# Layer 3 of a graph network: the attention sums moved behind the W_out step, and what follows them moved with them

## The chip, the cores and the metric

The kernel runs on one core of a Trainium2 chip. The metric is the device time of one execution in microseconds (us). The kernel before has a median of 2066.45 us in 3 runs (2065.35 to 2071.23).

## The reference

Four layers work on 32 images of 512 nodes with 64 features each. Layers 0 to 2 are not touched by the change. Layer 3 is a graph attention with 8 heads of width 128, followed by a second attention with one head of width 64 on the heads' output:

```
def gat_layer(x, graph, W, b):
    h = x @ W
    s = einsum('bnd,bmd->bnm', h, h) * graph
    s = where(s == 0.0, -1e16, s)
    a = softmax(s, axis=2)
    return einsum('bnm,bmd->bnd', a, h) + b

h = maximum(layernorm(x), 0)
heads = vmap(gat_layer)(Wh, bh)                 # 8 heads
cat = leaky_relu(concatenated heads, 0.01)
out = gat_layer(cat, graph, W_out, b_out)
x = x + leaky_relu(out, 0.01)
```

All numbers are float32.

## The kernel before

Layer 3 is cut into units. A unit is two attention matrices of 512 x 512 that are worked on side by side: for a `Heads` unit two heads of one image, for an `Out` unit the second attention of two images. There are 128 Heads units and 16 Out units, 144 in all. An Out unit is placed 7 or more units behind the last head that it needs; the last 8 units of the list are Out units.

The order of the instructions on all five queues is written out by hand: `period(t)` (inside `planned`, L702) is called for t = -1, 0, 1, ... and issues one step each of several units. `unit(lag)` is the unit that began `lag` periods ago, `now` is `unit(0)` and `ahead` is `unit(-1)`, the next one. The scheduler keeps this order on each engine, and adds the waits that the data and the buffers ask for. An engine takes its instructions in this order only. `ROOM = 6` periods after the last unit let it finish.

The steps of one unit, with the lines of the kernel before:

- `scores(r)` (L370, PE): for a block r of 128 rows, two score matrices of 128 x 512 into a PSUM tile of tag "s". This tag has two buffers of two banks.
- `maxima(r)` (L382, VectorE): masks the scores, negates them, keeps them in SBUF (`p`), and takes each row's extreme into `top`. Four row blocks give 8 instructions. Blocks 0 and 1 are done a period ahead, 2 and 3 in the unit's own period.
- `spread_out` and `spread_in` (L389, L392, L398): VectorE transposes `top`; four DMAs on SP write it to DRAM as a row, and one DMA on SP reads the row back to all 128 partitions (`topb`, 512 KB).
- `shift(r)` (L404, POOL): subtracts `topb` from a row block of `p`. The order of the blocks is 0, 2, 1, 3.
- `exps(r)` (L413, ACT): the exponential. Blocks 0 and 2 stay in SBUF, blocks 1 and 3 go to a PSUM tile of tag "s".
- `join(r)` for r = 1, 3 (L416, VectorE): adds block r to block r - 1. With it the values can be formed from differences of neighbours' features.
- `values(j)` (L422, PE): the attention's product with the features, four steps, into `av`.
- `totals` (L434, L440): PE sums the joined blocks 1 (e = 0) and 3 (e = 1) over the rows with a matrix of ones, into a PSUM tile; ACT copies it to SBUF (`tot`). This tile has tag "m" (two buffers) before.
- `totals_out` (L445): two small DMAs rearrange the sums to `parts`, one on ACT's queue and one on SP's.
- `recips`, `recips_out`, `recips_in` (L451, L454, L458, L465): VectorE adds the parts and takes reciprocals; a DMA on SP writes them to DRAM as a row; two DMAs on SP read them back to 64 partitions each (`recb`, 128 KB each).
- `normalize` (L471, VectorE): `av` times `recb` gives `o_att`.
- Heads: `y_pe` (L552, PE) multiplies with the head's weights into two tiles of tag "m"; `y_act` (L562, ACT) makes 0.01 times the value plus bias; `y_dve` (L570, VectorE) takes the larger of the two, which is the leaky relu.
- Out: `y_act` (L638, ACT) adds b_out in the kernel before; `back` (L643 PE, L648 ACT) transposes back and makes the 0.01 branch; `back_dve` (L651, VectorE) takes the larger; `back_pool` (L657, POOL) adds x; `store` (L664, SP) writes the result.
- `product(h)` (L597, PE): the W_out step, which gathers 8 heads of two images into `gT_ps`; `keep_product` copies it. `make_v` (L610), `make_gs` (L620), `judge_product` (L623) prepare an Out unit.
- `features`, `make_hx` (L298), `make_g` (L534, L546) prepare Heads units some periods ahead; `any_zero` gathers a test of the inputs' form, in the period after the last unit.

The period before issues on PE: scores of blocks 2 and 3 of `now`, sums of unit(2), scores of blocks 0 and 1 of `ahead`, y of unit(4), values of unit(2), W_out, then make_v, hx and g.

## Time and profile before

| | |
|---|---|
| median of the runs | 2066.45 us |
| the profiled execution's own time | 2070.2 us |
| its span, from the first to the last instruction | 2068.4 us |
| PE busy in the span | 1982.9 us |
| VectorE (DVE) busy | 1774.3 us |
| POOL busy | 1432.8 us |
| ACT busy | 1220.4 us |
| mean granted TensorE clock | 0.985 |
| start of the maxima of blocks 2, 3 of the first, third and last unit | 457.20, 478.12, 2019.60 us |

The busy times are of one profiled execution. A line of the timeline has the start in us from the span's start, the time, the engine, the line of the kernel, the operation, what is written from what, the number of instructions merged, and in brackets the idle time before it with what ended it. PEld is PE's loading of weights, which runs beside its matmuls. "SPq" and "ACTq" are DMA issues on SP's and ACT's queues.

### The profile page before, as it was taken

The numbers are of one execution on the slowest core, as the hardware profiler recorded it, in microseconds if no ns is written. First come the engines' busy times: TensorE is split into PE (matmuls) and PEld (weight loads), VectorE is DVE, ScalarE is ACT, GpSimd is POOL, SyncE is SP. The second block draws the span as 40 slices with busy tenths as digits, with TensorE's granted clock in tenths as the row PEclk, the third lists the DMA queues.
The fourth block names the chain that finished last, engine by engine and source line by source line (L and its number), as shares of the span: only waits on it lengthen the run. The fifth ranks groups of instructions, "written<-read, shape, count | busy, mean of one in ns | idle before, by whom it ended". The sixth has DMA issues, their size and how long they took to land. (4 is left out here: it accounts for less than half of the span.)

```text
span 2068.4 us, 32906 instructions
## 1 busy us (share of the span) xinstructions
PE 1982.9 (96%) x11038; PEld 808.1 (39%) x11038; DVE 1774.3 (86%) x4257; ACT 1220.4 (59%) x1944; POOL 1432.8 (69%) x697
## 2 busy tenths in 40 slices
PE   7999999997999999999999999999999999999995
PEld 4676776762333333333333333333333333333231
DVE  6699997676998889998989898989898898888993
ACT  3444443345666666766666667666666766666553
POOL 2000000008888989898888889888888888888995
PEclk9999999989999999999999999999999999999997
DMA  5000000001222222222222222222222222222222
GB/s 141 1 1 1 1 2 1 2 11 58 78 74 79 74 78 81 76 75 82 74 79 73 83 74 79 73 80 77 69 78 73 69 78 77 75 68 79 76 81 69
DMA packets 135778, 129.32 MB, mean 63 GB/s; under 512 B 92792, under 2 KB 98080, under 8 KB 135472
## 3 DMA queue, kind: packets, MB, share of 16 engines
q1 hardware_dynamic: 116368, 126.35, 20.5%
q10 hardware_dynamic: 18720, 0.59, 0.5%
q8 instruction: 88, 1.44, 0.3%
q0 software_dynamic: 512, 0.20, 0.1%
q14 instruction: 90, 0.74, 0.1%
HBM read 119.48 MB, written 5.37 MB: 60 GB/s over the span
## 5 line engine op out<-in xcount | busy, mean ns | idle before, releaser
L404 POOL TENSOR_TENSOR p_att<-p_att,topb 128x1024 f32<-128x1024 f32 x576 | 1347.8, 2375 | 202.1 <-DMA topb<-top_row 136.7
L382 DVE CUSTOM_DVE_ANT_0 p_att<-s_ps,flow_neg 128x512 f32<-128x512 f32 x1152 | 726.2, 686 | 74.4 <-PE s_ps L370 73.0
L370 PE MATMUL s_ps<-hx,g 64*128 64x512 f32 x2048 | 518.1, 615 | 21.8 <-DVE p_att L416 19.4
L413 ACT ACTIVATE p_att<-p_att 128x1024 f32<-128x1024 f32 x288 | 304.3, 1057 | 232.6 <-POOL p_att L404 219.9
L416 DVE TENSOR_TENSOR p_att<-e_ps,p_att 128x1024 f32<-128x1024 f32 x288 | 342.4, 1200 | 55.4 <-ACT e_ps L413 54.1
L413 ACT ACTIVATE e_ps<-p_att 128x1024 f32<-128x1024 f32 x288 | 295.1, 1028 | 122.1 <-POOL p_att L404 111.2
L370 PEld LDWEIGHTS s_ps<-hx,g 64*128 64x128 f32 x2048 | 174.9, 186 | 336.7 <-DVE top L382 170.5
L422 PE MATMUL av<-p_att,hd 128*64 128x512 f32 x1024 | 270.5, 607 | 0.4 <-DVE o_att L471 0.4
L422 PE MATMUL av<-p_att,hn 128*64 128x512 f32 x1024 | 264.0, 594 | 0.0
L1053 POOL TENSOR_TENSOR x<-x,bias_b 128x512 f32<-128x512 f32 x16 | 20.3, 1274 | 280.7 <-DVE hn L826 280.7
L570 DVE SCALAR_TENSOR_TENSOR cat<-y_ps,bh,cat 128x512 f32<-128x512 f32 x256 | 179.8, 744 | 0.0
L562 ACT ACTIVATE cat<-y_ps,bh 128x512 f32<-128x512 f32 x256 | 161.5, 682 | 30.1 <-PE y_ps L552 28.9
L434 PE MATMUL tot_ps<-p_att,ones 128*32 128x512 f32 x1152 | 154.0, 607 | 0.0
L552 PE MATMUL y_ps<-o_att,wh_sb 64*128 64x512 f32 x512 | 133.0, 590 | 0.0
L597 PE MATMUL gT_ps<-cat,wo_sb 128*64 128x512 f32 x512 | 131.6, 592 | 0.0
L422 PEld LDWEIGHTS av<-p_att,hn 128*64 128x64 f32 x1024 | 73.7, 137 | 146.9 <-issue 146.9
L422 PEld LDWEIGHTS av<-p_att,hd 128*64 128x64 f32 x1024 | 62.3, 136 | 166.6 <-issue 130.1
L977 PE MATMUL acc<-v,s 64*128 64x65 f32 x2048 | 123.8, 279 | 0.7 <-DVE s L963 0.4
L977 PEld LDWEIGHTS acc<-v,s 64*128 64x128 f32 x2048 | 120.9, 194 | 5.9 <-DVE o L993 1.2
L884 PE MATMUL nt_ps<-adj_t,hn 128*128 128x512 f32 x256 | 117.0, 600 | 0.8 <-DVE hn L848 0.8
L471 DVE TENSOR_TENSOR o_att<-av,recb 128x512 f32<-128x512 f32 x144 | 95.4, 663 | 23.8 <-DMA recb<-rec_row 23.1
L546 ACT COPY g<-g_ps 128x512 f32<-128x512 f32 x128 | 69.4, 589 | 71.6 <-PE g_ps L534 71.6
(181 smaller groups left out, 1987.0 us busy)
## 6 DMA issues: line engine op xcount, KB each, us to landing
topb<-top_row SPq DMA_DIRECT2D x144, 512.0 KB
recb<-rec_row SPq DMA_DIRECT2D x288, 128.0 KB
top_row<-top_t SPq DMA_DIRECT2D x576, 1.0 KB
out_dram<-y SPq DMA_DIRECT2D x32, 128.0 KB
x<-in_x_dram SPq DMA_DIRECT2D x3, 1024.0 KB
parts<-tot ACTq DMA_DIRECT2D x144, 4.0 KB
parts<-tot SPq DMA_DIRECT2D x144, 4.0 KB
rec_row<-rec_flow SPq DMA_DIRECT2D x144, 4.0 KB
```

Of the source, the lines that this page charges most:

```text
L370: nc.tensor.matmul(ps[:, k], lhsT=g[halves(k), r * P : (r + 1) * P], rhs=x[halves(k), :], start=True, stop=True,)
L382: nc.vector.tensor_tensor_reduce(out=self.p[r][:, k], in0=ps[:, k], in1=flow_neg[:, r], scale=-1.0, scalar=BIG, op0=OP.add, op1=OP.min, ac ...
L404: nc.gpsimd.tensor_tensor(self.p[r], self.p[r], self.topb, OP.subtract)
L413: nc.scalar.activation(to, self.p[r], AF.Exp, scale=-1.0)
L416: nc.vector.tensor_tensor(self.p[r], self.joined, self.p[r - 1], OP.add)
L422: nc.tensor.matmul(self.av[halves(k), :], lhsT=self.v(k, j) if j % 2 else self.less_next(k, j), rhs=self.p[j][:, k], start=(j == 0), stop= ...
L434: nc.tensor.matmul(ps[q : q + 32, :], lhsT=ones, rhs=self.p[2 * e + 1][:, k], start=True, stop=True,)
L552: nc.tensor.matmul(ps, lhsT=wh_sb[halves(k), 2 * self.i + k, :], rhs=self.o[halves(k), :], start=True, stop=True,)
L562: nc.scalar.activation(self.cat[:, k], self.y[k], AF.Identity, bias=bh01[:, h : h + 1], scale=0.01)
L570: nc.vector.scalar_tensor_tensor(self.cat[:, k], self.y[k], bh[:, h : h + 1], self.cat[:, k], op0=OP.add, op1=OP.max,)
L597: nc.tensor.matmul(self.gps[halves(k), :], lhsT=wo_sb[:, h, :], rhs=Heads.cat.pop((self.b + k, h)), start=(h == 0), stop=(h == H - 1),)
L977: nc.tensor.matmul(self.acc[k][:, r], lhsT=self.s[b // 2][halves(k), b % 2, r * P : (r + 1) * P], rhs=self.v[halves(k), b], start=(b == 0) ...
```

## The change

The change rewrites the order in `period`, and the steps that it moves:

- The sums of a unit (`totals`, `totals_out`) move from the second period after it, behind the first scores, to the first period after it, behind the joins, which on PE is behind the W_out step. Their PSUM tile has tag "s" now. Both DMAs of `totals_out` are on SP, behind `store`.
- `recips`, `recips_out` and `recips_in` of unit(2) come behind the transpose of `now`; the DMA of `recips_out` is issued by ACT, and `recips_in` stands behind `spread_in` on SP.
- `y_pe` and `y_act` take unit(3) instead of unit(4), and stand behind the scores of `now`. `y_dve`, `back_dve` (unit(3)) and `normalize` (unit(2) instead of unit(3)) stand behind the second join.
- Adding b_out is a step of its own, `bias`, at the start of the period. `back` takes unit(3), `back_pool` unit(4).
- The first three `features` steps come ahead of `store` and the second join in the text; on ACT they stand between the last exponential and the copy of the sums.
- `shift(0)` and `exps(0)` of a unit are issued at the end of its own period instead of at the start of the next. For the first unit (t = 1) all four shifts are on VectorE, behind the maxima.

```diff
-        def shift(self, r):
-            nc.gpsimd.tensor_tensor(self.p[r], self.p[r], self.topb, OP.subtract)
+        def shift(self, r, engine):
+            engine.tensor_tensor(self.p[r], self.p[r], self.topb, OP.subtract)
...
         def totals(self):
-            ps = ps_m.tile([P, N], F32, name="tot_ps", tag="m")
+            ps = ps_s.tile([P, 2, N], F32, name="tot_ps", tag="s")[:, 0]
...
-        def totals_out(self, e, queue):
+        def totals_out(self):
 
             rows = self.tot.rearrange("(k e r) n -> k e r n", k=2, e=2)
-            queue.dma_start(
-                self.parts[:, e], rows[:, e, 0].rearrange("k (g i) -> k g i", i=8)
-            )
+            for e in range(2):
+                nc.sync.dma_start(
+                    self.parts[:, e], rows[:, e, 0].rearrange("k (g i) -> k g i", i=8)
+                )
...
         def recips_out(self):
             self.rec_row = dram.tile([2, N], F32, name="rec_row")
-            nc.sync.dma_start(
+            nc.scalar.dma_start(
                 self.rec_row.rearrange("k (g i) -> (k g) i", i=8), self.rec
             )
...
-        def y_act(self):
+        def bias(self):
             nc.scalar.activation(self.o, self.o, AF.Identity, bias=b_out2, scale=1.0)
...
             for r in range(2, C):
                 now.scores(r)
-            unit(3).recips_in()
-            unit(1).shift(0)
-            unit(1).exps(0)
-            unit(2).totals()
-            unit(2).totals_out(1, nc.scalar)
+            unit(3).bias()
+            if t != 1:
+                unit(1).shift(2, nc.gpsimd)
+                unit(1).exps(2)
             u, h = products.get(t - 1, (None, 0))
             if u and h == H - 1:
                 u.keep_product()
-            unit(1).shift(2)
-            unit(1).exps(2)
+            unit(3).y_pe()
+            unit(3).back()
+            unit(3).y_act()
             for r in range(2, C):
                 now.maxima(r)
             now.spread_out()
-            unit(2).totals_out(0, nc.sync)
+            unit(2).recips()
+            unit(2).recips_out()
             now.spread_in()
+            unit(2).recips_in()
             for r in range(2):
                 ahead.scores(r)
-            unit(4).y_pe()
-            unit(4).y_act()
-            unit(3).normalize()
             for r in range(2):
                 ahead.maxima(r)
-            unit(4).back()
-            unit(4).y_dve()
-            unit(4).back_dve()
-            unit(1).shift(1)
-            unit(1).exps(1)
+            if t == 1:
+                for r in (0, 2, 1, 3):
+                    unit(1).shift(r, nc.vector)
+                    if r < 3:
+                        unit(1).exps(r)
+            else:
+                unit(1).shift(1, nc.gpsimd)
+                unit(1).exps(1)
             for j in range(C):
                 unit(2).values(j)
             u, h = products.get(t, (None, 0))
             if u:
                 u.product(h)
-            unit(2).recips()
-            unit(2).recips_out()
             unit(1).join(1)
-            unit(1).shift(3)
+            if t != 1:
+                unit(1).shift(3, nc.gpsimd)
             unit(1).exps(3)
-            unit(5).back_pool()
+            unit(4).back_pool()
             unit(-2).make_gs()
+            for step in range(3):
+                for lag, odd in ((step - 7, 0), (step - 11, 1)):
+                    u = unit(lag)
+                    if getattr(u, "i", None) == 0 and u.b % 2 == odd:
+                        u.features(step)
             unit(5).store()
             unit(1).join(3)
+            unit(3).y_dve()
+            unit(3).back_dve()
+            unit(2).normalize()
+            unit(1).totals()
+            unit(1).totals_out()
             unit(-3).features(3)
             unit(-2).judge_product()
             unit(1).make_v()
             unit(-4).make_hx()
             unit(-2).make_g()
-            for step in range(3):
-                for lag, odd in ((step - 7, 0), (step - 11, 1)):
-                    u = unit(lag)
-                    if getattr(u, "i", None) == 0 and u.b % 2 == odd:
-                        u.features(step)
+            if t:
+                now.shift(0, nc.gpsimd)
+                now.exps(0)
             if t == len(units):
                 any_zero()
```

More of the change, by code (lines that the diff above doesn't have):

```diff
@@ L345, in y_pe @@
             pass
+        def bias(self):
+            pass
         def y_act(self):
@@ L635, in less_next, with bias @@
             return self.gD[:, j // 2, halves(k)]
-        def y_act(self):
+        def bias(self):
             nc.scalar.activation(self.o, self.o, AF.Identity, bias=b_out2, scale=1.0)
```

## The prediction

> **What bounds the kernel now.** I read the table of busy shares and the slices first, then the groups of PE, then the timelines of single engines over two periods of layer 3. Layer 3 fills the time from about 455 us to the end, 144 units in as many periods. In the page PE is the fullest engine there, with POOL behind it:
>
> ```profile
> PE 1982.9 (96%) x11038; PEld 808.1 (39%) x11038; DVE 1774.3 (86%) x4257; ACT 1220.4 (59%) x1944; POOL 1432.8 (69%) x697
> ...
> PE   7999999997999999999999999999999999999995
> ```
>
> The busy times over 478.1 to 2019.6 us (from unit 2's maxima to unit 143's) say it closer: PE 1512.92 of 1541.50 us in 141 periods, so a period is 10.93 us, of which 10.73 are PE's. The period is PE's work, nearly gap for gap. One period on PE:
>
> ```profile
> 1208.46 1.99 PE L370 MATMUL s_ps<-gs 64*128 64x512 f32 x8
> 1210.38 1.06 PE L434 MATMUL tot_ps<-p_att,ones 128*32 128x512 f32 x8
> 1211.37 1.99 PE L370 MATMUL s_ps<-hx,g 64*128 64x512 f32 x8
> 1213.19 1.02 PE L552 MATMUL y_ps<-o_att,wh_sb 64*128 64x512 f32 x4
> 1214.15 1.08 PE L422 MATMUL av<-p_att,hd 128*64 128x512 f32 x4
> ...
> 1217.63 1.03 PE L597 MATMUL gT_ps<-cat,wo_sb 128*64 128x512 f32 x4
> 1218.59 1.13 PE L534 MATMUL g_ps<-hx,m 64*128 64x512 f32 x4
> 1219.55 1.88 PE L370 MATMUL s_ps<-hx,g 64*128 64x512 f32 x8
> ```
>
> The first column is the start, the second the time. W_out (gT_ps) ends near 1218.6. The reader is to hold that against the second join of the same period, in VectorE's timeline; POOL's and ACT's give what leads to it:
>
> ```profile
> 1198.92 0.69 DVE L382 CUSTOM_DVE_ANT_0 p_att<-s_ps,flow_neg 128x512 f32<-128x512 f32 x1 [0.51 <-PE s_ps L370]
> ...
> 1201.48 0.21 DVE L389 STREAM_TRANSPOSE top_t<-top 128x32 f32<-128x32 f32 x1
> ...
> 1218.69 1.22 DVE L416 TENSOR_TENSOR p_att<-e_ps,p_att 128x1024 f32<-128x1024 f32 x1 [0.54 <-ACT e_ps L413]
> ```
>
> ```profile
> 1208.23 9.37 POOL L404 TENSOR_TENSOR p_att<-p_att,topb 128x1024 f32<-128x1024 f32 x4 [1.34 <-DMA topb<-top_row]
> ```
>
> ```profile
> 1217.63 1.03 ACT L413 ACTIVATE e_ps<-p_att 128x1024 f32<-128x1024 f32 x1 [1.20 <-POOL p_att L404]
> ```
>
> This is one unit's way: its maxima of rows 2, 3 start at 1198.92; the transpose ends at 1201.69; the row goes out and comes back, and POOL starts at 1208.23; its four shifts end at 1217.60; exp to 1218.66; the second join to 1219.91. That is 20.99 us, and no piece waits for another engine's queue. Taken the same way for units 10 to 129 the median is 20.95, and the smallest of all units 20.38. So the second join ends 1.3 us after W_out has ended on PE, and 0.36 us after the next unit's scores began. Before, nothing on PE needs it that early: the sums follow one period later.
>
> **What the Trainium skill says.** "PSUM — Partial Sum Buffer", section "Engine vs sequencer instructions": queues are strict FIFO, and matmuls start and complete in program order, so PE can't take the next scores past a sum that waits. The trace agrees so far: PE stands still behind such a wait (17.7 us in all ahead of back_ps, for o_att) with other work queued. "Perfetto Trace Analysis", section "Identifying the Most-Contended Engine": matmul busy time is no measure of the distance to the roofline. I use PE's busy time only as the length of its queue. "DMA: Bandwidth & Descriptors", section "Issuing engines are not separate DMA queues": issuing from another engine saves only the sequencer's issue time. Here that is 0.34 us (rec_row on SP); the 2.02 us from its issue (1206.37) to recb's (1208.39) stay.
>
> **The change, part by part.**
>
> *Sums behind W_out (totals, lag 2 to 1).* PE's new order is: scores 2, 3; y; scores 0, 1 of the next unit; values; W_out; sums of the unit just joined; hx, g or gV; next scores. The work is the same, but a wait is added: sums for e=1 need the second join, and the whole PE queue stands behind it, first of all the next period's scores, from which that unit's maxima come. Two periods thus close a loop. Its parts:
> - maxima to second join: 20.85 (median 20.95; POOL gets slack, so a little less; the ends are 20.4 and 21.2).
> - join to PE: 0.05.
> - sums for e=1: 0.9. All eight take 0.99; the pair for e=0 runs ahead, but the pair left is four instructions like the av group's (1215.06 to 1215.91, 0.85). The ends are 0.5 and 1.0.
> - hx, g, gV before the next scores: hx 0.6 x32, g 0.96 x64, gV 0.6 x16, over 144 = 0.63; g shares PSUM tag m with y, whose largest-of-two now runs after the join (0.74 x2), so its second matmul can wait some 0.3 us; 0.7 in all. The ends are 0.63 and 1.4 (g falls on every other period, and if neighbours can't even it out the loop with it rules).
> - scores start to maxima start: 1.1 (1219.55 to 1220.62, 1208.46 to 1209.63).
> Sum 23.6, so 11.8 us a period against 10.93: +0.87. From unit 3 to unit 143 are 140 periods: +122 us.
>
> *What could hide this?* PE's queue before the sums is 9.2 us long, so nothing covers the wait. Its cover today is the period between join and sums, and that is what the change gives up.
>
> *Sums in ps_s.* Seven tiles of tag s a period instead of six, with two buffers. Scores of row 3 now wait for the copy of the sums on ACT. Sums end + 0.2 + 0.58 (copy) against one scores pair, 0.96: covered. features stands ahead of that copy now (about 1.3 us from the end of exp 3; the join takes 1.22 and the sums 0.9): covered, and costs some 0.3 us in the few periods with two steps of it. I take 0.
>
> *parts, both on SP behind store.* 2 x 0.57 us of issue. They leave spread_out's neighbourhood, where one lay between top_row and topb; but topb was issued 0.32 us after it (1214.61 to 1214.93), waiting for top_row's landing. I take 0 for that, 0.3 as the best. parts lands some 2 us after issue, about 0.5 us before recips stands at the head of VectorE: covered; if late, the maxima of rows 0, 1 start later, and those have 2 us until the joins.
>
> *recips to behind the transpose, rec_row on ACT behind y_act, recb right after topb on SP.* ACT's queue gains 0.5 us; exp 1 behind it has its shift at about the same time. recb stands behind topb, 512 KB. From the second shift: exp 1.05, cat 1.27, issue 0.5, landing 1.5, recb issue and landing 4.3 (2053.26 to 2057.03 in the last unit, 3.8, and 0.5 for topb), division 0.65. With maxima to second shift 13.8 that is 23.1 to the next-but-one maxima, 0.5 us under the loop: covered, but next in line.
>
> *Largest-of-two and division behind the joins.* 2 x 0.7 + 0.6 us on VectorE between join 3 and maxima: 20.85 + 2.0 = 22.9, under 23.6: covered by the sums, hx/g and scores on PE.
>
> *Bias early, shift 0 at the period's end.* POOL's cyclic order is unchanged. The 17.7 us that PE stands before back_ps vanish only where PE sets the period; here they are inside the new wait: 0.
>
> *Ramp.* Unit 0's four shifts move to VectorE. Price by "VectorE: DVE Perf Modes", section "The TRN2 errata — SBUF-src ops pay a fixed extra latency per instruction", (N+151)/0.96 for a fp32 tensor_tensor: an estimate of 1.22 us for N=1024; no row shows this one, the join's 1.20 us with a PSUM operand is near. 4.9 us instead of POOL's 9.26; the ends are 4.4 and 6. The second join of unit 0 ends near 475.2 instead of 478.2, and unit 1's shifts need no longer queue: unit 3's maxima come at 462.68 + 23.6 = 486.3 instead of 489.38: -3.1.
>
> *Tail.* Last unit: maxima 2019.60, span's end 48.8 later. Its sums' copy ended 27.7 after the maxima, because PE had earlier values and back to do. Now it is join 20.9 + 0.9 + 0.8 = 22.6; from there the chain is the same but for 0.6 us of the second issue: -5.
>
> *Sum.* 122 - 3 - 5 = +114 on the profiled 2070.2 us (span 2068.4), that is 2184. The median of the runs is 3.75 lower, 2066.45: **2180 us**.
>
> **Rivals.**
> - *Faster.* If the join came within 2 x 10.73 - 2.75 = 18.7 us of the maxima, PE would not wait: the period falls to PE's 10.73, taking out the 28.6 us that PE idles between 478.1 and 2019.6, with ramp and tail 2066 - 28 - 8 = 2030 us. One mechanism, topb landing 2.1 us sooner with parts out of its way on SP. For it: POOL waits for topb in most periods (1.34 us above). Against: topb waits for top_row, not for SP, and no unit of 144 is under 20.38. 5%.
> - *Milder.* All low ends: 20.4 + 0.05 + 0.5 + 0.7 + 1.1 = 22.75, 11.4 a period, +63 - 8: about 2121 us. 16%.
> - *Heavier.* g and PSUM tag m in one of the two loops, or recb late by a microsecond and division holding the maxima: 24.6, 12.3 a period, +192 - 8: about 2250 us. 15%.
> - *No effect.* The order of the instructions would have to come out as before on PE; it doesn't, the sums do stand behind W_out. Gains and waits cancel by accident: 2%.
>
> **How the numbers follow.** The forecast, 2150 to 2215, has 62%; the milder case fills 2110 to 2150, the heavier 2215 to 2260. Leaving out the faster cases and half the heavier gives 2115 to 2235. Faster by over 0.3% (about what a measurement of this kernel can tell from no change, 6 us) 0.05, within 0.02, slower 0.93.
>
> **What would show it.** Right: PE's idle time ahead of tot_ps with the join (L416's successor) as releaser, about 1 us a period; PE's busy share in layer 3 near 91%; maxima to join still near 20.9; POOL waiting for topb about 2 us a period; cat's wait for y gone. Wrong: the join under 19 us from the maxima, or PE idle ahead of scores (PSUM, copy of the sums) or VectorE idle ahead of recips or division (parts, recb) instead of ahead of tot_ps.

## The result, and the profile after

The changed kernel takes 2259.82 us (median of 4 runs, 2247.58 to 2261.84) against 2066.09 us before on the same chip (2065.35 to 2071.23): ratio 1.0917, 95% interval 1.0879 to 1.0954. The direction was forecast, the size was not: 2180 us was the forecast, and the result lies above its range, where the rival "heavier" had put 2250 us.

The profiled execution has a span of 2256.5 us. First the page's lines on TensorE's busy time and its slices:

```profile
PE 2103.6 (93%) x11038; PEld 863.6 (38%) x11038; DVE 1787.9 (79%) x4261; ACT 1226.1 (54%) x1944; POOL 1421.2 (63%) x693
...
PE   7999999979999999999999999999989999999996
```

PE is busy 120.7 us more than before with the same 11038 matmuls. The profile models where a matmul ends, so part of a matmul's wait for a late operand is counted as busy time. The groups of instructions show where, first of the kernel before, then of the one after. After the first bar stand the busy time in us and the mean time of one instruction in ns; after the second, the idle time in us just before the group, and who ended most of it.

```profile
L434 PE MATMUL tot_ps<-p_att,ones 128*32 128x512 f32 x1152 | 154.0, 607 | 0.0
```

```profile
L437 PE MATMUL tot_ps<-p_att,ones 128*32 128x512 f32 x1152 | 247.4, 608 | 77.8 <-DVE p_att L419 69.3
```

The sums took 154.0 us of PE and now take 247.4 + 77.8 = 325.2: 171 us more, of a span that grew by 188.1. The join (L419) ends the wait. Here is one period in PE's timeline (start, us, engine, line; in brackets the idle time before it); hold it against the PE lines in the prediction:

```profile
1210.17 1.99 PE L373 MATMUL s_ps<-hx,g 64*128 64x512 f32 x8
1211.99 1.02 PE L556 MATMUL y_ps<-o_att,wh_sb 64*128 64x512 f32 x4
1212.88 2.35 PE L373 MATMUL s_ps<-hx,g 64*128 64x512 f32 x8
...
1218.65 1.03 PE L601 MATMUL gT_ps<-cat,wo_sb 128*64 128x512 f32 x4
1219.61 1.05 PE L437 MATMUL tot_ps<-p_att,ones 128*32 128x512 f32 x4
1221.71 1.05 PE L437 MATMUL tot_ps<-p_att,ones 128*32 128x512 f32 x4 [1.05 <-DVE p_att L419]
1222.69 1.46 PE L538 MATMUL g_ps<-hx,m 64*128 64x512 f32 x4
1223.66 2.21 PE L373 MATMUL s_ps<-hx,g 64*128 64x512 f32 x8
```

And this is VectorE's timeline for the unit that meets those sums:

```profile
1200.50 0.69 DVE L385 CUSTOM_DVE_ANT_0 p_att<-s_ps,flow_neg 128x512 f32<-128x512 f32 x1 [1.15 <-PE s_ps L373]
...
1220.43 1.22 DVE L419 TENSOR_TENSOR p_att<-e_ps,p_att 128x1024 f32<-128x1024 f32 x1 [1.10 <-ACT e_ps L416]
1221.57 1.40 DVE L574 SCALAR_TENSOR_TENSOR cat<-y_ps,bh,cat 128x512 f32<-128x512 f32 x2
1222.89 0.68 DVE L475 TENSOR_TENSOR o_att<-av,recb 128x512 f32<-128x512 f32 x1
1225.05 0.69 DVE L385 CUSTOM_DVE_ANT_0 p_att<-s_ps,flow_neg 128x512 f32<-128x512 f32 x1 [1.47 <-PE s_ps L373]
```

The maxima start at 1200.50 and the second join ends at 1221.65: 21.15 us. The second half of the sums starts on PE when the join ends, then come g and the scores, and the maxima of the next unit but one start at 1225.05: 24.55 us for two periods. That is the forecast's loop, with both halves longer. Over units 10 to 129 two periods take 24.68 us in the mean: 21.41 from maxima to second join, 3.27 from there to the maxima (before: 21.17 and 0.70). A line of POOL and two of SP's queue show one reason for the first half:

```profile
1209.99 7.02 POOL L407 TENSOR_TENSOR p_att<-p_att,topb 128x1024 f32<-128x1024 f32 x3 [4.30 <-DMA topb<-top_row]
```

```profile
1205.54 0.34 SPq L401 DMA_DIRECT2D topb<-top_row  x1
1205.98 1.18 SPq L469 DMA_DIRECT2D recb<-rec_row  x2
```

From topb's issue to the start of POOL, which waits for it, the median is 4.28 us; before, when recb was not issued right behind it, it was 3.85. The waits from 600 to 2000 us (who waited, for whom: us in total, times, longest) name the others:

```profile
PEld tot_ps L437 <- DVE p_att L419: 186.7, 161, 2.2
...
ACT e_ps L416 <- DVE top L385: 59.9, 75, 1.8
...
DVE o_att L475 <- DMA recb<-rec_row: 50.8, 48, 3.0
PEld g_ps L538 <- DVE cat L574: 39.4, 47, 0.8
```

The exponentials to PSUM wait for maxima that free their tile, the division waits for recb, and g waits for a PSUM buffer that the larger-of-two (cat) frees.

**An account of TensorE.** Every step of a period passes through PE's one queue, so a mean period can be written as the sum of what each step holds PE: its modelled busy time and the idle time ahead of it, each moment counted once (from the trace, 600 to 2000 us, in us; W_out is in "values"; the last column holds the Out units' transposes and gV). Such a sum comes out for any kernel. It shows at which step PE's time went; why it went there is for the waits and the experiments to say.

| kernel | period | sums | scores | y | g | HX | values | transposes |
|---|---|---|---|---|---|---|---|---|
| before | 10.93 | 0.99 | 3.89 | 0.81 | 0.49 | 0.13 | 4.40 | 0.22 |
| after | 12.34 | 2.11 | 4.00 | 0.92 | 0.66 | 0.14 | 4.36 | 0.14 |

Of the 1.41 us that were added, the sums hold 1.12 and g 0.17. The same account is used on the experiments below.

### The profile page after: what moved, and what is told of

Same layout as the page of the kernel before. It is cut to its first block, busy times and chain, and to the rows that moved or that the text cites. A ratio compares the mean times of both kernels' runs of the same rounds, so it can differ in the third digit from the quotient of the medians.

```text
span 2256.5 us, 32811 instructions
## 1 busy us (share of the span) xinstructions
PE 2103.6 (93%) x11038; PEld 863.6 (38%) x11038; DVE 1787.9 (79%) x4261; ACT 1226.1 (54%) x1944; POOL 1421.2 (63%) x693
## 4 chain that ended last, share of the span: by engine, by line
PE 33%; POOL 24%; DMA 14%; DVE 14%; issue 9%; ACT 4%; SPq 2%; POOLq 0%; DVEq 0%; ACTq 0%
POOL p_att L407 24%; DMA topb<-top_row 9%; DVE p_att L385 7%; PE nt_ps L897 7%; PE acc L990 5%; PE s_ps L373 4%; PE tot_ps L437 4%; DVE p_att L419 3%; PE av L425 3%; PE g_ps L538 3%; ACT e_ps L416 2%; DMA top_row<-top_t 2%; DMA recb<-rec_row 2%; PE po L917 1%; SPq L395 1%
## 5 line engine op out<-in xcount | busy, mean ns | idle before, releaser
L373 PE MATMUL s_ps<-hx,g 64*128 64x512 f32 x2048 | 558.1, 617 | 14.1 <-DVE top L385 3.2
L419 DVE TENSOR_TENSOR p_att<-e_ps,p_att 128x1024 f32<-128x1024 f32 x288 | 352.6, 1225 | 171.1 <-ACT e_ps L416 169.5
L437 PE MATMUL tot_ps<-p_att,ones 128*32 128x512 f32 x1152 | 247.4, 608 | 77.8 <-DVE p_att L419 69.3
L373 PEld LDWEIGHTS s_ps<-hx,g 64*128 64x128 f32 x2048 | 202.4, 186 | 302.1 <-DVE top L385 189.5
L443 ACT COPY tot<-tot_ps 128x512 f32<-128x512 f32 x144 | 84.4, 586 | 257.9 <-PE tot_ps L437 215.1
L556 PE MATMUL y_ps<-o_att,wh_sb 64*128 64x512 f32 x512 | 154.3, 599 | 7.9 <-DVE o_att L475 7.8
L437 PEld LDWEIGHTS tot_ps<-p_att,ones 128*32 128x32 f32 x1152 | 35.8, 108 | 275.4 <-DVE p_att L419 239.4
```

Of the source, the lines that this page charges most:

```text
L373: nc.tensor.matmul(ps[:, k], lhsT=g[halves(k), r * P : (r + 1) * P], rhs=x[halves(k), :], start=True, stop=True,)
L419: nc.vector.tensor_tensor(self.p[r], self.joined, self.p[r - 1], OP.add)
L437: nc.tensor.matmul(ps[q : q + 32, :], lhsT=ones, rhs=self.p[2 * e + 1][:, k], start=True, stop=True,)
L556: nc.tensor.matmul(ps, lhsT=wh_sb[halves(k), 2 * self.i + k, :], rhs=self.o[halves(k), :], start=True, stop=True,)
```

## The experiments

The theory to test: the sums' wait for the second join closes a loop of two periods, and g and recb make it longer than forecast. The rival: the rest of the new order carries the loss. Some of these kernels leave out recb, its row and its broadcast and multiply by a constant instead; they serve for timing alone. Each group of runs has its own runs of the kernel before, whose median went from 2066 to 2073 us; across groups ratios are compared.

### Parts of the change on the kernel before

*Sums alone.*
```diff
-            ps = ps_m.tile([P, N], F32, name="tot_ps", tag="m")
+            ps = ps_s.tile([P, 2, N], F32, name="tot_ps", tag="s")[:, 0]
...
-            unit(2).totals()
-            unit(2).totals_out(1, nc.scalar)
...
-            unit(2).totals_out(0, nc.sync)
...
             unit(1).join(3)
+            unit(1).totals()
+            unit(1).totals_out(1, nc.scalar)
+            unit(1).totals_out(0, nc.sync)
```


> Kernel before with one part of the change: the sums of a unit behind its joins, on PE behind W_out (tag s). Everything else is as before. Loop theory (sums wait for the second join, the next scores wait for the sums, so two periods hold maxima-to-join 21.0 + 2.2 and, in the slower of the two interleaved loops, g 0.96): 24.1 in two periods, about 12.05 each, so about 2220 us, and PE idle ahead of tot_ps. Rival (recb right behind topb on SP, and the division that waits for it, are what slows the changed kernel): none of that is here, so 2066 us within 0.5%.

2396.39 us, ratio 1.1582 (1.1565 to 1.16): slower than the whole change, and far above the 2220 us of the loop theory. In the old order recb is issued by SP behind the parts, which wait for the sums, and the division stands ahead of the first maxima, so that these wait as well:

```profile
DVE o_att L471 <- DMA recb<-rec_row: 67.7, 100, 2.7
```

The same kernel without recb, in the square further down, takes 2289.00 us; so recb's way is worth about 110 us of this loss.

*Bias early and ramp on VectorE.*
```diff
             unit(3).recips_in()
+            unit(4).bias()
...
+            if t == 1:
+                for r in (0, 2, 1, 3):
+                    unit(1).shift(r, nc.vector)
+                    if r < 3:
+                        unit(1).exps(r)
```


> Kernel before with two parts of the change that don't touch the sums: b_out added at the start of the period, and the first unit's four shifts on VectorE. Loop theory: the sums are alone to blame, so these parts cost nothing: 2045 to 2063 us (up to 17.7 us of PE's idle time ahead of back_ps go, and about 3 us of the ramp). Rival (these parts carry a part of the slowdown, as bias ahead of the exponentials on ACT or the ramp, where the changed kernel gained nothing): 2066 us or more.

2059.92 us, ratio 0.9949 (0.9935 to 0.9962).

*Bias alone.*


> The kernel before with only the bias issued at the start of its period, ahead of the exponentials, instead of behind the W_out product. Splits the 6 us that the bias and the VectorE ramp gained together. If the bias (which ends the 17.7 us in which TensorE's transposes wait for ScalarE, 0.12 us a period) is the source: 2056 to 2062 us. If the ramp is (its first maxima came 1.2 us earlier): 2064 to 2066 us.

2062.92 us, ratio 0.9945 (0.9927 to 0.9964). So the bias is the gain, and the ramp adds nothing that can be told. Both versions beat the kernel before and the changed one: between 600 and 2000 us PE's idle time falls from 0.18 us a period to 0.11 and 0.13, and none of it stands before the transposes any more.

### One cost taken out of the changed kernel

*No recb.*
```diff
-            nc.vector.tensor_tensor(self.o, self.av, self.recb, OP.mult)
+            nc.vector.tensor_tensor(self.o, self.av, urow, OP.mult)
...
-            unit(2).recips_out()
...
-            unit(2).recips_in()
```


> Changed kernel without the way of the reciprocals: rec_row and recb are left out, and the division multiplies by a constant tile (so the output isn't divided by the sums). Loop theory: only topb gets back the 0.43 us that it takes longer with recb behind it, and single late divisions go; the loop stays: 2215 to 2240 us. Rival (recb and the wait for it): the periods fall to 11.4 or less, 2130 us or less.

2222.51 us, ratio 1.0733 (1.0708 to 1.0759). The time from topb's issue to POOL's start falls to 3.80 us, maxima to join to 21.14, join to maxima to 3.05. So recb's way cost 38 us (from the ratios), and the forecast had it covered.

*HX and g first.*
```diff
                 now.scores(r)
+            unit(-4).make_hx()
+            unit(-2).make_g()
...
             unit(1).make_v()
-            unit(-4).make_hx()
-            unit(-2).make_g()
```


> Changed kernel with make_hx and make_g directly behind the period's first scores, instead of behind the sums. Loop theory with the slower of two loops ruling: g (0.96, and up to 0.3 of waiting for y's buffers) and hx leave the stretch from join to maxima, 24.6 falls to about 23.5 in two periods: about 2175 to 2190 us. If the extras were evened out between the loops (as the prediction took them): 0.35 us a period, about 2210. Rival (recb, division): 2250 us, no change.

2215.97 us, ratio 1.0705 (1.0688 to 1.0722): not the 2175 to 2190 of a slower loop that rules alone, but near the 2210 of loops that even out. The two periods got 0.65 us shorter, but y now stands behind g and shares its PSUM buffers.

*Both.*


> The changed kernel with both the earlier edits at once: recb, its row and its broadcast left out (the division multiplies by a constant tile), and the HX and g steps issued directly behind the first scores. If the two costs add along the two-period chain (2222.5 - 2259.8 = -37 and 2216.0 - 2259.8 = -44): 2170 to 2185 us, a period of about 11.75. If they only uncover each other, as when each loop's other wait is next in line: 2205 or more. If the two together hide each other's next-in-line wait (the slower loop governs): below 2160.

2186.80 us, ratio 1.0542 (1.0516 to 1.0568). The two gains add, within the noise.

*Sums that don't wait* (and no recb).
```diff
-            unit(2).recips()
...
+            unit(3).recips()
...
-            unit(1).totals()
-            unit(1).totals_out()
+            unit(2).totals()
+            unit(2).totals_out()
```


> The changed kernel, with the ones sums of the unit before the last (joined one period earlier) at the same place behind the joins; the reciprocals follow one unit later, and the division multiplies by a constant tile instead of recb, whose row and broadcast are left out. TensorE issues the same matmuls in the same places, but none of them waits for a join of its own period. Loop theory (the two-period chain join, sums, maxima is the cost): the period falls back to what TensorE's work needs, 10.75 to 10.95 us, so 2035 to 2065 us in all. Rival (the rest of the new order is what costs: larger-of-two and division behind the joins, sums in the scores' PSUM ring): the period stays at 11.6 or more, 2150 us or more.

2251.08 us, ratio 1.0867 (1.084 to 1.0895). This is against my theory in its simple form: the wait is gone, and against "no recb" nothing is gained; the ratios are 28 us apart the other way. Those 28 us can't be put down to the order, because the granted TensorE clock was lower here: 0.967 to 0.974 in the four executions, against 0.987 to 0.989. If PE's clock had set every moment of the period, that would be 0.018 of 2251, about 40 us (an estimate from these clocks). Even so this kernel would be at 2210, level with "no recb" and far from the 2035 to 2065 of the theory. The groups show why; first the sums, then g and HX:

```profile
L437 PE MATMUL tot_ps<-p_att,ones 128*32 128x512 f32 x1152 | 153.4, 605 | 11.1 <-DVE p_att L419 10.6
```

```profile
L538 PE MATMUL g_ps<-hx,m 64*128 64x512 f32 x256 | 121.2, 714 | 78.9 <-DVE cat L574 78.8
...
L298 PE MATMUL hx_ps<-ident,hs 128*128 128x128 f32 x128 | 21.9, 298 | 22.9 <-DVE cat L574 22.9
```

The sums are back at about their old 154 us. Now g and HX wait for buffers of tag "m" that the larger-of-two frees, and the larger-of-two was moved behind the same join.

*Sums that don't wait, HX and g first* (and no recb).


> The changed kernel with three edits: sums of the unit before the last at the same place, constant instead of recb in the division (its row and broadcast left out), HX and g directly behind the first scores. Seen from the run with sums that don't wait, where the loss stayed, there are three more ways by which the next first scores or maxima wait for the second join: the sums take a tile of the scores' PSUM ring of two, so the first scores take the tile that the second join frees; g takes a buffer that the larger-of-two, now behind the joins, frees; and on VectorE the larger-of-two (1.40) and the division (0.68) stand between join and maxima. Parallel-paths theory: with the sums' operand wait and g's wait out, VectorE's own order still gives 21.2 + 2.2 = 23.4 in two periods, 11.7 a period: 2155 to 2190 us, level with the 2186.8 of the same kernel whose sums do wait. Rival (two waits at once were hiding the gain): below 2120.

2171.04 us, ratio 1.0478 (1.0445 to 1.0512), where the theory of parallel paths put it. But in the account below, its period is 0.76 us above the kernel before, and y alone holds 0.76 more (1.57 instead of 0.81), since it waits for ACT to copy g and so free the buffers:

```profile
PEld y_ps L556 <- ACT g L550: 103.1, 111, 3.4
```

So this is a new hole, not the proof of VectorE's order that I expected; the number agreed by luck.

### The sums put back, the rest left

*Sums back; sums back without recb; the same with HX and g first.* The sums of unit(2) go back to tag "m" early in the period, parts on ACT and SP as before:
```diff
                 unit(1).exps(2)
+            unit(2).totals()
+            unit(2).totals_out(1, nc.scalar)
...
+            unit(2).totals_out(0, nc.sync)
             now.spread_in()
-            unit(2).recips_in()
...
                 ahead.maxima(r)
+            unit(2).recips()
+            unit(2).recips_out()
+            unit(2).recips_in()
...
-            unit(1).totals()
-            unit(1).totals_out()
```


> The changed kernel with only the sums put back: the ones sums of the unit before the last early in the period in their old PSUM ring, their parts on ScalarE's and SyncE's queues as before, reciprocals behind the first maxima, and recb issued by SyncE last in the period. Early bias, VectorE ramp, larger-of-two and division behind the joins stay. Loop theory: no TensorE work waits for this period's joins, the period is TensorE's own 10.7 to 10.9 us, and the tail keeps part of its gain: 2035 to 2065 us, level with or a little under the kernel before. Rival (the rest of the order carries part of the loss): 2100 or more.

> The changed kernel with the sums back early in the period in their old PSUM ring, and the division multiplying by a constant tile (recb, its row and broadcast left out), so that of the change only the larger-of-two and division behind the joins, the early bias and the ramp are left. Parallel-paths theory: VectorE's order gives 21.2 + 2.2 and the g step still waits for the larger-of-two in every second period, 23.4 to 24.2 in two periods: 2160 to 2230 us. Rival (the sums alone are the cause): below 2080.

> The same with HX and g directly behind the first scores: no TensorE work waits for the second join by operand, by the scores' ring's shift or by g's buffers. Left is VectorE's own order: join, larger-of-two 1.40, division 0.68, maxima. If that alone is enough: 21.0 to 21.2 + 2.2, 11.65 a period, 2140 to 2190 us. If TensorE's waits were the whole cause: below 2080. The sums and the W_out product now stand behind g's copies, which may add some tenths a period.

2485.86, 2402.52 and 2291.06 us (ratios 1.1975, 1.1586, 1.1045): all three far above both theories. Sums and y are now both ahead of the next unit's first scores, y takes the tile that the sums free, and ACT, which must copy the sums first, stands behind an exponential. This is PE in the second of them:

```profile
1198.48 1.06 PE L437 MATMUL tot_ps<-p_att,ones 128*32 128x512 f32 x8
1199.47 1.12 PE L555 MATMUL y_ps<-o_att,wh_sb 64*128 64x512 f32 x2
1202.66 0.87 PE L555 MATMUL y_ps<-o_att,wh_sb 64*128 64x512 f32 x1 [2.07 <-ACT tot L443]
```

The granted clock was lower in these three as well (0.945 to 0.980). They can't tell what the parts of the change cost; they show that a step can't be put back alone.

### The larger-of-two and the division back, then the sums elsewhere

From "sums that don't wait, HX and g first"; bias, y and transposes follow one period later:
```diff
             now.spread_out()
+            unit(3).normalize()
...
                 ahead.maxima(r)
+            unit(4).y_dve()
+            unit(4).back_dve()
...
             unit(1).join(3)
-            unit(3).y_dve()
-            unit(3).back_dve()
-            unit(2).normalize()
```


> The run with sums that don't wait, HX and g first and no recb (2171.0), with the larger-of-two and the division taken from behind the joins to their old places in the next period (W_out product, bias and transposes one period later with them). Left of the ways from the second join to the next maxima is the scores' PSUM ring alone: join, first scores, maxima, some 1.2 us. Parallel-paths theory: 21.1 + 1.2 = 22.3 in two periods, 11.15 a period, 2075 to 2110 us. Rival (VectorE's two instructions were covered, and something else holds the 11.7 us period): 2155 or more.

2182.17 us, ratio 1.054 (1.0518 to 1.0562). Join to maxima fell to 1.28 us as expected, but maxima to join rose to 22.28. The rival was right on the time. The first join starts 19.92 us after the maxima, 1.53 later than in the kernel that this one starts from: the larger-of-two now stands ahead of it on VectorE. That place alone is not enough, for the last kernel below has the larger-of-two there too, and its maxima to join is 20.99. Here y also waits for g's copies (it holds PE for 1.39 us a period), the next unit's first scores stand behind y, and their maxima start 5.01 us after those of the current unit, against 3.63 in that last kernel.

And with the sums moved from there into tag "m":
```diff
                 ahead.scores(r)
+            unit(2).totals()
+            unit(2).totals_out()
...
-            unit(2).totals()
-            unit(2).totals_out()
```


> The same with the sums taken out of the scores' PSUM ring too (old ring, behind the first scores of the next unit): none of the ways from the second join to the next scores or maxima is left; the division still multiplies by a constant, recb left out. Theory: the period is TensorE's own again, 10.75 to 11.0 us, 2045 to 2080 us. Rival (a cost outside these paths, say ScalarE's or SyncE's order): 2100 or more.

2682.70 us, ratio 1.2955 (1.2929 to 1.2981). The sums, in the old ring behind the next unit's first scores, wait for the larger-of-two of the same period, and ACT's copy of them stands ahead of the exponentials:

```profile
1204.81 1.93 PE L437 MATMUL tot_ps<-p_att,ones 128*32 128x512 f32 x8 [2.43 <-DVE cat L574]
```

The granted clock fell too, to 0.905: in the stretch of this line the trace has it at 0.50, and the eight matmuls take 1.93 us instead of 1.06. So this run says nothing on the theory that it was made for.

### A square on the kernel before

These four have the sums behind the second join, and no recb. They differ in two questions. Are the sums those of the unit just joined, or of the one before it (does the operand wait)? And is their PSUM tile in the scores' ring of two tiles, tag "s", or in the old one, tag "m" (do the first scores take the tile that the second join frees)? This is the one with neither:
```diff
-            unit(3).recips_in()
...
-            unit(2).totals()
-            unit(2).totals_out(1, nc.scalar)
...
-            unit(2).totals_out(0, nc.sync)
...
             unit(1).join(3)
+            unit(2).totals()
+            unit(2).totals_out(1, nc.scalar)
+            unit(2).totals_out(0, nc.sync)
```


> The kernel before with only the sums moved behind the joins into the scores' PSUM ring; the division multiplies by a constant tile, recb, its row and its broadcast are left out. Larger-of-two and division stay early. Parallel-paths theory: the sums alone make the loop, join 21.0, sums 0.9, HX/g/gV 0.6, scores to maxima 1.1: 23.6 in two periods, 11.8 a period, 2165 to 2205 us (the 2396 of the same kernel with recb came from recb standing behind the late parts on SyncE's queue). Rival (larger-of-two and division carry the loss, sums none): below 2090.

> The kernel before, with the sums of the unit before the last (joined a period ago) issued behind the second join and in the scores' PSUM ring; the division multiplies by a constant, recb, its row and broadcast left out. No TensorE operand waits for this period's join; only the ring is shifted by one tile, so that the first scores take the tile that the second join frees. If the ring's shift alone is enough to close the loop: a period of 11.5 to 12.4, 2140 to 2290 us. If it is not: 2050 to 2080.

> The same, with the sums in their old PSUM ring: same matmuls, same place behind the second join, neither the operand nor the scores' ring waits for it. Theory (the loss is in the waits, not in the sums' place or number): level with the kernel before, 2050 to 2080 us. Rival (matmuls between the joins and the first scores cost their own time on the path wherever they wait): 2120 or more.

> The kernel before, with the sums of the unit just joined behind the second join, as in the change, but in their old PSUM ring; constant in the division, recb left out. Only the operand waits for the join; the scores' ring is not shifted. If the operand's wait alone closes the loop, as TensorE's order says: 2165 to 2290 us, level with the 2289.0 of the same kernel in the scores' ring. If the ring is the cause: 2050 to 2090.

| | operand waits | operand doesn't wait |
|---|---|---|
| scores' ring | 2289.00 (1.1041: 1.1009 to 1.1073) | 2187.00 (1.0574: 1.0554 to 1.0594) |
| old ring | 2329.54 (1.1263: 1.1243 to 1.1283) | 2228.03 (1.0769: 1.0747 to 1.0791) |

Both kernels whose operand waits came out above what was expected of them. "Neither" should have been level with the kernel before and is 7.7% slower: the theory that the waits on the join are all of it fell here. Its rival, that matmuls between the joins and the first scores cost their own time, named the right range, but in the account the sums hold 1.00 us there as before; the scores and g hold more. The square is additive: the operand's wait costs 97 (from the ratios) and 102 us, and the scores' ring is better than the old one, by 46 us where the operand waits (from the ratios) and 41 where it doesn't (in the old ring g waits for the copy of the sums, and holds 0.87 instead of 0.56). What all four share is seen in PE's timeline of "neither":

```profile
1208.43 1.06 PE L434 MATMUL tot_ps<-p_att,ones 128*32 128x512 f32 x8
...
1210.82 2.25 PE L370 MATMUL s_ps<-hx,g 64*128 64x512 f32 x7
1213.70 2.26 PE L370 MATMUL s_ps<-hx,g 64*128 64x512 f32 x8 [0.64 <-DVE top L382]
```

Between the two groups of scores PE waits for maxima to free a tile of the ring. Before, the sums stood there and filled that time. Taken away, they leave a hole: in all four the scores hold 4.76 to 4.80 us instead of 3.89, and 0.87 x 140 periods are 122 us, about the 119 that "ring only" (scores' ring, no waiting operand) lost. In the changed kernel y has been moved into that place, and its scores hold 4.00.

### Both waits taken away, no matmul moved

From "sums that don't wait", with one edit:
```diff
                 ahead.maxima(r)
+            unit(3).y_dve()
+            unit(3).back_dve()
...
             unit(1).join(3)
-            unit(3).y_dve()
-            unit(3).back_dve()
```


> The run with sums that don't wait (2251.1; no recb, constant in the division), with one edit: the larger-of-two goes back in front of the joins, behind the first maxima, while the division stays behind them. Then neither the sums nor g wait for the second join, and no matmul has changed its place, so TensorE gets no new hole. Account of TensorE's time per period for the run it starts from: 12.24, of it g 0.80 busy and 0.59 idle before it where the kernel before has 0.49, and HX 0.35 where it has 0.13. If the two waits are the loss: 12.24 - 0.90 - 0.22 = 11.1, with the scores' ring and later joins 0 to 0.2 more: 2065 to 2115 us. Rival (another wait takes over, as in every run so far): 2150 or more.

2106.72 us, ratio 1.0165 (1.0148 to 1.0182), inside what the account gave. Sums, scores and g of this kernel:

```profile
L373 PE MATMUL s_ps<-hx,g 64*128 64x512 f32 x2048 | 535.2, 616 | 40.1 <-DVE p_att L419 30.6 <-DVE top L385 1.9
L437 PE MATMUL tot_ps<-p_att,ones 128*32 128x512 f32 x1152 | 153.4, 605 | 16.7 <-DVE p_att L419 16.3
...
L538 PE MATMUL g_ps<-hx,m 64*128 64x512 f32 x256 | 78.6, 646 | 0.0
```

No group but the scores waits much now, and those wait for the second join: the sums take a seventh tile of the ring, so the first scores take the tile that this join frees. The account of the runs that decide:

| kernel | period | sums | scores | y | g | HX | values | transposes |
|---|---|---|---|---|---|---|---|---|
| no recb | 12.09 | 2.09 | 3.86 | 0.80 | 0.67 | 0.14 | 4.40 | 0.15 |
| HX and g first | 12.01 | 1.37 | 3.94 | 1.57 | 0.49 | 0.14 | 4.38 | 0.14 |
| both | 11.82 | 1.22 | 3.92 | 1.56 | 0.47 | 0.14 | 4.39 | 0.11 |
| sums don't wait | 12.24 | 1.09 | 3.99 | 0.88 | 1.39 | 0.35 | 4.38 | 0.15 |
| the same, HX and g first | 11.69 | 1.00 | 3.99 | 1.57 | 0.47 | 0.14 | 4.38 | 0.13 |
| sums and g free | 11.26 | 1.12 | 4.14 | 0.82 | 0.51 | 0.13 | 4.39 | 0.16 |
| square: ring only | 11.76 | 1.00 | 4.76 | 0.80 | 0.56 | 0.14 | 4.38 | 0.11 |
| square: neither | 12.09 | 1.00 | 4.78 | 0.80 | 0.87 | 0.14 | 4.39 | 0.12 |

Down the column of the sums, then g and HX: freeing the sums alone moves 1.0 us from one column to the next (g and HX from 0.81 to 1.74); freeing both gives it back. From "sums don't wait" to "sums and g free" the ratio falls by 0.070, 145 us, of which up to 40 can be the lower clock of the first. "No recb" and this kernel ran at the same clock (0.986 to 0.989), and from one to the other the ratio falls by 0.0568, 118 us.

So the loss of 9.2% comes apart like this: about 38 us go with recb, 118 with the waits of the sums and of g behind the second join, which have to be taken away together, and 34 us (1.65%) are left. All the rest of the new order, y, bias, parts and division, is still in that last kernel, so it can carry no more than what is left, unless a gain hides a part of it.

## Why the prediction was wrong

Right in it was the mechanism: sums of the unit just joined make PE's queue stand at the second join, with g and the next scores behind it. What the Trainium skill says in "PSUM — Partial Sum Buffer", section "Engine vs sequencer instructions", that matmuls start and complete in program order, agrees with the trace of after: 1.05 us idle before the sums at 1221.71, with g and the scores behind them. The wait of about 1 us a period that was to show before tot_ps is there: 0.48 as idle time, and 1.12 with what the profile counts as busy. That is also why PE's busy share between the maxima of units 3 and 143 is 94% and not the 91% that were to show.

Wrong were terms of the sum, "maxima to second join", "hx, g, gV before the next scores" and "recb: covered". The rival "heavier" had two of the reasons: g and its PSUM buffers in one loop, recb holding the division. With maxima of unit 3 at 490.38 and of unit 143 at 2214.12, a period is 12.31 us instead of 11.8. 140 times 0.51 are 71 us, the ramp missed by 4, the tail the other way by 1. Together these are the 74 us between the span that the steps gave (2068.4 + 114) and 2256.5.

- **"maxima to second join: 20.85"** measured 21.41, above its range of 20.4 to 21.2. Of the 0.56 us, 0.22 were there before the change: the forecast started from the median of the units, 20.95, but the periods add up to the mean, and that was 21.17. Another 0.10 is the gain from POOL's slack, which did not come. The rest goes with recb: issued 0.44 us behind topb, it makes POOL start 0.43 us later after topb's issue, and without it the mean is 21.14.
- **"hx, g, gV before the next scores: 0.7"** is the other mis-sized term. With nothing between sums and scores and no late division, join to maxima is 2.21 us, the shortest of all (2.05 in the forecast); the mean is 3.27, so 1.06 stands for the 0.7. In the 50 units with g alone it is 3.40, the 0.96 of g's matmuls and some 0.2 for the buffers that cat frees. The forecast spread g over all periods, and had the loop with g only as its upper end, 1.4. But in the 34 units with none of the three it is 2.97 and not 2.21, because there the division is late. Without recb it is 2.39 there.
- **"recb ... covered, but next in line"** was wrong. In 33 of the 34 units with neither hx, g nor gV between the sums and the scores, VectorE's division comes late because it waits for recb (48 such waits in all between 600 and 2000 us, up to 3.0 us), and recb also delays POOL. Together this is the 38 us above.
- **"Largest-of-two and division behind the joins: covered"** held only as it was put, under the sums. Once the sums no longer wait, the place of the larger-of-two costs 145 us, or some 105 if all of the lower clock is taken off. The forecast knew the PSUM buffers that the larger-of-two frees for g, but sized that wait at some 0.3 us and counted the rest by VectorE's queue (22.9). With the sums' cover gone, g and HX hold 0.93 us a period more.
- **"Sums in ps_s: 0"** held for ACT's copy. That the first scores take the second join's tile was not seen. This costs nothing that shows while the sums wait for the same join (scores 3.86 in "no recb"), and some 0.2 us a period when neither the sums nor g do (30.6 us in all in the last kernel, scores 4.14).
- **"The work is the same"** is true of the changed kernel only because y went where the sums had been. The square shows what that place is worth, 0.87 us a period.
- **Parts on SP: 0**: nothing speaks against it; topb is issued 5.33 us after the maxima (5.49 before).
- **Bias: 0**: no run takes it out of the changed kernel, where PE still waits 10.6 us before back_ps between the maxima of units 3 and 143 (the 17.7 of the prediction, before). Alone on the kernel before it gains 0.55%.
- **Ramp: -3.1** measured +1.0. Unit 0's second join ended at 475.54, as worked out (475.2). But on PE the sums of unit 0 now stood ahead of unit 2's scores (and took 3.01 us, at a granted clock of 0.50), and on ACT unit 1's exponentials then waited for maxima:

```profile
474.50 3.01 PE L437 MATMUL tot_ps<-p_att,ones 128*32 128x512 f32 x8 [8.33 <-POOL p_att L407]
477.44 2.81 PE L373 MATMUL s_ps<-hx,g 64*128 64x512 f32 x8
```

```profile
483.77 1.03 ACT L416 ACTIVATE e_ps<-p_att 128x1024 f32<-128x1024 f32 x1 [3.73 <-DVE top L385]
```

  The sums were moved in the ramp too, and the step was costed without them. Where they stay, in "bias early and ramp", the maxima of unit 3 come at 488.18, 1.2 us earlier than before.
- **Tail: -5** measured -6.4 (42.4 us from the last maxima to the end, 48.8 before).

What stays open: how the 0.33 us a period that "sums and g free" still has over the kernel before is shared between the ring, the late sums and the joins; and what the larger-of-two costs alone on the kernel before, which no run shows cleanly. What "sums and g free" would take with recb in was not tried. No run here shows why the granted clock differed between these kernels.

## What to carry to other kernels

Where one in-order engine is busy for most of the period, keep an account of it by step, busy and idle before each. It told in every run here where the time was, while most theories on loops missed. Compare the granted clocks first. When a step is moved, ask three things of the account: what it will wait for in the new place, which other step waits for the same event and so takes over when the first wait is cured, and what hole it leaves in the place it had. A wait that is "covered" by another has to be listed with the buffers that it frees, not only with its engine's time.

## What the runs showed of the hardware

Two DMAs of a broadcast of 256 KB in all (recb), issued 0.44 us behind a broadcast of 512 KB (topb), went with a later start of the POOL instruction that waits for topb: 4.28 us after topb's issue in the median. It was 3.80 without recb, and 3.85 before, where recb was issued 4.0 us after topb.

Four subtractions of 128 x 1024 float32 from SBUF on VectorE have records of 1.22 us each, which is the estimate of the prediction from the Trainium skill's "VectorE: DVE Perf Modes", section "The TRN2 errata — SBUF-src ops pay a fixed extra latency per instruction". But they start 1.14 us apart, so the four took 4.62 us and not 4.9. On POOL the same instruction takes 2.37 us.

In the kernel of 2682.70 us (the larger-of-two and the division back, the sums in tag "m") the trace has 67 stretches of 3.4 or 6.8 us at half the TensorE clock between 600 and 2000 us, 294 us in all; the changed kernel has none there.
